# A four-layer graph network on one core: the deviation as exp(-0.5 ln v), two layers normalised on GpSimd, another beginning and another end

## The chip, the core and the metric

The kernel runs on one core of a Trainium2 chip. The core has a matrix engine (TensorE, PE in the profile), a vector engine (VectorE, DVE), an engine for functions of one element (ScalarE, ACT), a general engine (GpSimd, POOL), and a queue (SyncE, SP) that issues most of the transfers between the chip's main memory and the on-chip memories: SBUF, 128 partitions wide, and PSUM, where matrix products arrive. Each engine works through its own list of instructions in order; semaphores make one engine wait for another. The metric is the device time of one execution in microseconds (us), lower is better. Most executions agree within 0.3%.

## The reference, cut to what matters

Thirty-two graphs `x[b]` of 512 nodes with 128 features go through four layers with one shared adjacency matrix. Every layer adds its result to its input and normalises each node's 128 features.

```python
def _layernorm(x, axis=-1, eps=1e-5):
    m = jnp.mean(x, axis=axis, keepdims=True)
    v = jnp.var(x, axis=axis, keepdims=True)
    return (x - m) / jnp.sqrt(v + eps)

# layers 0 and 1: attention over neighbours
h = x @ W
e = leaky_relu((h @ a_src)[i] + (h @ a_dst)[j], 0.2)
out = softmax(where(adj > 0, e, -big)) @ h        # 0: + b, leaky_relu(0.3);  1: elu
# layer 2: own features times W[0], mean over the other neighbours times W[1], + bias
# layer 3: y = (adj @ x + x) @ weight + bias;  y = y / max(norm(y), 1e-12)

x = _layernorm(x + L0(x)); x = _layernorm(x + L1(x))
x = _layernorm(x + L2(x)); x = _layernorm(x + L3(x))
```

## The kernel before, in words

A graph is one tile of 128 partitions by 512 elements: four quarters ("chunks", `NCH` = 4) of 128 nodes, each 128 by 128. The work on a graph is cut into *units*, small functions that issue one or a few instructions on one engine. `@unit("nrm0", ...)` gives a unit's name and its tiles.

The order of everything is written out by hand. `PLAN` gives for each unit and each of the 32 graphs a position (-1: not run), `STARTS` does it for the units that run once. The units are issued in the order of these positions, which interleaves many graphs; an engine's own list is what of it falls to that engine. Tiles come from pools of fixed size (six PSUM banks, thirty SBUF tiles `sq`), in turn.

The steps of a graph, with their lines in the profile:

- `ld` (L150) loads the graph. Its transpose is made on PE with `pt0` (L167) and copied from PSUM with `xt0` (L171), which before does for graph 0 only; for graphs 1 to 31 `lb` (L156) loads it a second time in blocks of 32 by 32, four transfers per graph, and `tr0` (L160) transposes the blocks on DVE.
- Layers 0 and 1: `ph` (L179) multiplies by W and the attention vectors, `ex` (L183) takes exponentials on ACT, `h` (L189) scales. The row of exponentials gets to all partitions either through PE (`pr`, L209, for graphs 0, 1, 2, 30 and 31) or through main memory (`rt`, `rw`, `rb`, L214 to L224). `al` (L236) makes the attention matrix on DVE with four instructions of 128x512, `po` (L196) multiplies on PE, `rs`, `v0`, `v1`, `lr`, `exp`, `elu` finish.
- Layers 2 and 3: `xh`, `xl` (L273 on ACT, L277 on POOL) split the features in two parts, `py` (L284) aggregates, `y` (L288) copies, `po2`, `po3` (L298, L299, L311) multiply by the weights, `v2`, `v3` (L305, L315) add the bias on DVE. In layer 3, `sq` (L321) takes squares and their sums on ACT, `ssp` (L325, L326) takes the maximum with 1e-24 and the power -0.5 on POOL, `rr0` to `rr3` (L333) scale and add the input on DVE.
- Normalising: `add0`, `add1` (L267) and `xb` (L292) are additions on POOL. `bn` takes statistics on DVE (L340, L342): mean and variance plus eps of each node. `ms` (L346) changes the mean's sign on ACT, `pw` (L350, L351) takes the power -0.5 of the variance on POOL and multiplies it by the negative mean, and `nrm` (L356) applies scale and shift on ACT, one instruction for each chunk.
- `st` (L361) stores the graph with one transfer.

Units that run once prepare the masks (`e`, `am`, `m`, `mp`, `cva`, `cvd`, L439 to L473), weights (`awt`, `awc`, `awq`, `aws`, L418 to L433; `wb` loads those of layer 1), biases (`rest`, L412), and warm PE with transposes that nobody reads (`warm`, `warm2`, L401, L406). `de` (L500 to L502) compares the values of the row `eb`, and `out_d` (L507 to L512) collects doubts about the inputs; if there are any, a general path runs at the end, which here does not happen.

Of the kernel before, what the change touches and what calls it, by code (L numbers as in the profile page):

```python
# [14 lines left out]
AF = mybir.ActivationFunctionType  # L15
# [3 lines left out]
P = 128  # L19
# [7 lines left out]
def kernel(  # L27
# [120 lines left out]
    @unit("ld", "x0")  # L148
    def _(b, x0):
        nc.sync.dma_start(chunks(x0), x[b].rearrange("(c p) f -> p c f", p=P))  # L150
# [11 lines left out]
    for k in range(3):  # L162

        @unit(f"pt{k}", f"x{k}", f"pt{k}")
        def _(b, xk, p):
            for c in range(NCH):
                nc.tensor.transpose(p[:, c * P : (c + 1) * P], xk[:, c * P : (c + 1) * P], ident)  # L167

        @unit(f"xt{k}", f"pt{k}", f"xt{k}")
        def _(b, p, xt):  # L170
            nc.scalar.copy(xt, p)  # L171
# [151 lines left out]
    @unit("ssp", "ss")  # L323
    def _(b, ss):
        nc.gpsimd.tensor_scalar(ss, ss, 1e-24, None, op0=ALU.max)  # L325
        nc.gpsimd.tensor_tensor(ss, ss, mhalf, op=ALU.pow)  # L326
# [8 lines left out]
    for k in range(4):  # L335
# [8 lines left out]
        @unit(f"ms{k}", f"mv{k}")  # L344
        def _(b, mv):
            nc.scalar.mul(mv[:, :, 0], mv[:, :, 0], -1.0)  # L346

        @unit(f"pw{k}", f"mv{k}", f"rn{k}")
        def _(b, mv, rn):
            nc.gpsimd.tensor_tensor(rn[:, 0], mv[:, :, 1], mhalf, op=ALU.pow)  # L350
            nc.gpsimd.tensor_mul(rn[:, 1], mv[:, :, 0], rn[:, 0])  # L351
# [6 lines left out]

    @unit("st", "x4")
    def _(b, x4):  # L360
        nc.sync.dma_start(out[b].rearrange("(c p) f -> p c f", p=P), chunks(x4))  # L361

    for n in ("aw0", "aw1", "aq0", "aq1", "pf", "pm0", "pm1", "pm2", "pm3", "pflag"):
        KIND[n] = "ps"
# [10 lines left out]
    def first():  # L375
# [6 lines left out]
        nc.scalar.activation(bad[:, 0:1], minus1, AF.Exp)  # L382
# [15 lines left out]
    @unit("warm", "pf")  # L398
    def _(b, p):
        for i in range(12):  # L400
            nc.tensor.transpose(p[:, :P], ident, ident)  # L401

    @unit("warm2", "pf")
    def _(b, p):
        for i in range(8):
            nc.tensor.transpose(p[:, :P], ident, ident)  # L406
# [112 lines left out]
    def _(b, p):  # L519
# [3 lines left out]
        "ja": 1, "warm": 2, "wb": 3, "awt0": 4, "warm2": 5, "awc0": 6, "e2": 7, "e0": 10, "rest": 11, "am2": 12,  # L523
        "e1": 13, "awq0": 14, "aws0": 16, "am0": 17, "e3": 18, "eh": 20, "am1": 21, "awt1": 22, "am3": 23,
        "awc1": 24, "m2": 26, "m3": 27, "awq1": 29, "m0": 30, "m1": 31, "cva2": 33, "aws1": 34, "mp": 35, "cva1": 38,
        "cvd2": 39, "de": 42, "cva3": 45, "cvd1": 46, "cvd3": 48, "cva0": 51, "cvd0": 54, "dga": 55, "deg": 61,
        "lpp": 239, "lpd": 274, "dv": 420, "out_d": 2455, "out_p": 2530, "out_c": 2533,
    }
    PLAN = {
        "ld": [0, 8, 9, 49, 52, 89, 137, 181, 215, 292, 362, 432, 502, 563, 642, 724, 797, 860, 928, 1006, 1070, 1163,  # L530
            1211, 1280, 1378, 1438, 1526, 1601, 1694, 1944, 1770, 1839],
        "pt0": [15, -1, -1, -1, -1, -1, -1, -1, -1, -1, -1, -1, -1, -1, -1, -1, -1, -1, -1, -1, -1, -1, -1, -1, -1, -1,
            -1, -1, -1, -1, -1, -1],
        "xt0": [19, -1, -1, -1, -1, -1, -1, -1, -1, -1, -1, -1, -1, -1, -1, -1, -1, -1, -1, -1, -1, -1, -1, -1, -1, -1,
            -1, -1, -1, -1, -1, -1],
        "ph0a": [32, 64, 73, 91, 117, 129, 201, 249, 309, 348, 419, 483, 561, 669, 741, 831, 906, 980, 1059, 1143,
            1215, 1298, 1388, 1479, 1568, 1664, 1723, 1797, 1890, 1957, 2059, 2121],
        "ph0b": [25, 60, 67, 94, 116, 125, 175, 218, 263, 345, 415, 486, 562, 670, 713, 775, 864, 929, 1020, 1103,
            1190, 1270, 1351, 1441, 1500, 1569, 1697, 1749, 1830, 1905, 1995, 2086],
        "ex0a": [36, 69, 77, 95, 122, 144, 203, 256, 316, 353, 424, 491, 564, 675, 748, 835, 912, 984, 1064, 1147,  # L540
            1221, 1304, 1397, 1483, 1576, 1671, 1730, 1804, 1894, 1966, 2064, 2130],
        "ex0b": [37, 65, 72, 97, 120, 131, 183, 232, 277, 349, 423, 492, 567, 678, 719, 785, 873, 936, 1025, 1107,
            1195, 1274, 1359, 1451, 1509, 1575, 1700, 1759, 1835, 1913, 1999, 2091],
        "pc0": [43, 75, 80, 101, 123, 148, 204, 264, 322, 356, 427, 497, 570, 683, 751, 837, 915, 992, 1066, 1153,
            1226, 1309, 1401, 1489, 1581, 1673, 1736, 1809, 1899, 1968, 2068, 2133],
        "pr0": [40, 70, 79, -1, -1, -1, -1, -1, -1, -1, -1, -1, -1, -1, -1, -1, -1, -1, -1, -1, -1, -1, -1, -1, -1, -1,
            -1, -1, -1, -1, 2076, 2136],
        "h0a": [47, 76, 81, 102, 124, 153, 206, 265, 328, 357, 429, 499, 572, 684, 752, 843, 916, 1000, 1072, 1157,
            1265, 1339, 1432, 1490, 1584, 1683, 1741, 1822, 1903, 1970, 2069, 2141],
        "h0b": [50, 78, 82, 104, 133, 160, 205, 278, 330, 361, 440, 505, 574, 688, 758, 850, 945, 1005, 1076, 1159,  # L550
            1227, 1310, 1403, 1492, 1587, 1688, 1747, 1829, 1911, 1972, 2081, 2158],
        "al0": [44, 74, 87, -1, -1, -1, -1, -1, -1, -1, -1, -1, -1, -1, -1, -1, -1, -1, -1, -1, -1, -1, -1, -1, -1, -1,
            -1, -1, -1, -1, 2083, 2151],
        "po0a": [58, 85, 96, 178, 197, 240, 301, 358, 405, 534, 575, 617, 698, 800, 872, 952, 1038, 1120, 1206, 1284,
            1368, 1453, 1528, 1607, 1701, 1774, 1846, 1952, 2022, 2096, 2166, 2238],
        "po0b": [53, 90, 109, 185, 189, 234, 312, 363, 396, 545, 585, 639, 734, 807, 878, 983, 1060, 1150, 1224, 1318,
            1394, 1486, 1540, 1650, 1725, 1786, 1871, 1940, 2034, 2111, 2185, 2258],
        "rs0a": [66, 92, 110, 187, 210, 251, 310, 369, 448, 550, 590, 646, 726, 812, 886, 974, 1051, 1136, 1238, 1302,
            1382, 1465, 1550, 1621, 1709, 1777, 1865, 1961, 2030, 2107, 2176, 2247],
        "rs0b": [59, 98, 127, 192, 211, 252, 326, 383, 418, 558, 597, 649, 746, 818, 899, 995, 1077, 1164, 1239, 1334,  # L560
            1409, 1498, 1551, 1662, 1737, 1796, 1882, 1953, 2049, 2126, 2199, 2279],
        "v0a": [68, 99, 114, 190, 214, 259, 311, 374, 455, 554, 592, 666, 731, 819, 901, 979, 1086, 1141, 1243, 1307,
            1387, 1469, 1553, 1623, 1717, 1782, 1870, 1963, 2032, 2108, 2181, 2253],
        "v0b": [71, 103, 130, 198, 216, 262, 327, 394, 458, 573, 609, 668, 753, 827, 904, 997, 1088, 1168, 1245, 1340,
            1413, 1503, 1556, 1669, 1743, 1800, 1887, 1977, 2052, 2128, 2204, 2285],
        "lr": [86, 107, 136, 207, 227, 270, 329, 409, 464, 586, 658, 722, 762, 846, 907, 1018, 1091, 1173, 1248, 1366,
            1416, 1521, 1591, 1674, 1765, 1814, 1934, 1997, 2071, 2139, 2214, 2291],
        "add0": [88, 112, 143, 213, 235, 282, 342, 425, 476, 594, 665, 733, 779, 859, 917, 1021, 1102, 1188, 1275,
            1377, 1433, 1525, 1599, 1686, 1769, 1827, 1943, 2008, 2088, 2143, 2222, 2305],
        "bn0": [93, 118, 156, 222, 245, 300, 379, 430, 490, 612, 687, 739, 815, 887, 954, 1037, 1123, 1203, 1315, 1389,  # L570
            1460, 1538, 1616, 1711, 1778, 1860, 1955, 2020, 2097, 2161, 2237, 2323],
        "ms0": [100, 132, 163, 228, 260, 304, 388, 439, 504, 620, 690, 749, 820, 892, 965, 1045, 1134, 1219, 1342,
            1398, 1467, 1545, 1645, 1718, 1787, 1868, 1960, 2033, 2104, 2167, 2250, 2330],
        "pw0": [105, 135, 166, 229, 266, 307, 390, 445, 509, 623, 691, 754, 822, 896, 970, 1047, 1138, 1222, 1349,
            1402, 1470, 1547, 1654, 1722, 1790, 1883, 1969, 2060, 2112, 2173, 2261, 2333],
        "nrm0": [113, 145, 174, 236, 281, 320, 402, 453, 517, 632, 701, 768, 828, 905, 988, 1057, 1152, 1230, 1353,
            1420, 1476, 1552, 1659, 1733, 1795, 1895, 1978, 2073, 2123, 2180, 2269, 2340],
        "pt1": [121, 151, 194, 247, 296, 331, 411, 471, 544, 645, 711, 778, 869, 962, 1044, 1117, 1200, 1294, 1363,
            1434, 1522, 1811, 1699, 1753, 1852, 1937, 2018, 2122, 2196, 2192, 2293, 2349],
        "xt1": [128, 155, 196, 257, 302, 337, 417, 479, 546, 651, 712, 788, 876, 969, 1052, 1121, 1205, 1299, 1371,  # L580
# [462 lines left out]
```

## Time and profile before

| | |
|---|---|
| time, median of 3 runs | 582.84 us (580.44 to 582.96) |
| the profiled execution | 582.73 us |
| its span, first to last instruction | 581.0 us |
| busy: PE, DVE, ACT, POOL | 547.7, 526.0, 503.6, 427.0 us |
| POOL's powers (L350) | 128 of 1053 ns, 134.7 us |
| ACT's normalisations (L356) | 512, 209.5 us |
| table loads on ACT | 1, 1283 ns |
| PE's last instruction ends | 566.5 us |

A row of the profile names a line of the kernel, its engine and operation, the tiles (`out<-in`) and the shape; "x128" is the number of instructions. Busy time counts overlapping instructions once. "Idle before" is time in which the engine stood still just before such an instruction, and the arrow names what ended it. The profile is of one execution, so sums are made against its span.

### The profile page before, as it was taken

To read this page: it belongs to the slowest core of one execution; us is meant where nothing else is said; L and a number is where in the kernel's file an instruction comes from. 1 tells how busy PE (TensorE), PEld (TensorE's weight loads), DVE (VectorE), ACT (ScalarE), POOL (GpSimd) and SP (SyncE) were. 2 spreads that over 40 slices of the span, in tenths; PEclk is the share of its full clock that TensorE was granted. 3 is DMA by queue.
4 is the path that set the end of the run, shared out by engine and by line. 5 is a ranking of instruction groups with operands and counts; after the bars stand their busy time and mean duration, and the time that the engine had idled before them with its cause. 6 is when DMAs were issued, how large, how long until landed. Compare 5 with 4: busy or idle time off the path is not lost.

```text
span 581.0 us, 13866 instructions
## 1 busy us (share of the span) xinstructions
PE 547.7 (94%) x4200; PEld 516.1 (89%) x4200; DVE 526.0 (91%) x2005; ACT 503.6 (87%) x1653; POOL 427.0 (73%) x578
## 2 busy tenths in 40 slices
PE   7799999899999999999999999999999999999980
PEld 6689999899999999999999989898998999998860
DVE  2688979899999999999998999999999999779674
ACT  4555598798989899999999889899988999998996
POOL 3151685787868787777878579776887779789985
PEclk9788999999999999999999999999999999999995
DMA  6616022323434334352432343332201111000013
GB/s 188 130 38 128 19 60 70 92 65 83 99 77 101 77 70 110 92 117 55 104 78 76 83 97 74 66 101 73 75 20 38 55 38 38 20 2 20 1 37 113
DMA packets 111296, 41.84 MB, mean 72 GB/s; under 512 B 69872, under 2 KB 103792, under 8 KB 111216
## 3 DMA queue, kind: packets, MB, share of 16 engines
q1 hardware_dynamic: 110640, 40.57, 29.2%
q8 instruction: 35, 0.57, 0.4%
q14 instruction: 45, 0.37, 0.2%
q10 hardware_dynamic: 576, 0.33, 0.2%
HBM read 32.38 MB, written 8.50 MB: 70 GB/s over the span
## 4 chain that ended last, share of the span: by engine, by line
DVE 35%; PE 33%; ACT 16%; POOL 5%; SPq 4%; issue 3%; DMA 2%; ACTq 0%; DVEq 0%; POOLq 0%
PE ps L196 16%; DVE al L236 12%; ACT sq L356 8%; PE ps L284 7%; DVE st L340 6%; PE ps L179 4%; DVE sq L333 3%; DVE sq L305 2%; SPq L156 2%; DVE mv L342 2%; DVE sq L243 2%; ACT hp L189 2%; PE ps L167 2%; PE ps L311 2%; DVE sq L253 2%
## 5 line engine op out<-in xcount | busy, mean ns | idle before, releaser
L196 PE MATMUL ps<-hp,al 128*128 128x129 f32 x2048 | 251.2, 279 | 6.4 <-DVE al L236 4.4
L196 PEld LDWEIGHTS ps<-hp,al 128*128 128x128 f32 x2048 | 243.1, 195 | 10.0 <-issue 3.1
L356 ACT ACTIVATE sq<-sq,rn 128x128 f32<-128x128 f32 x512 | 209.5, 492 | 12.8 <-POOL rn L351 12.6
L350 POOL TENSOR_TENSOR rn<-mv,mhalf 128x4 f32<-128x4 f32 x128 | 134.7, 1053 | 22.1 <-DVE mv L342 15.4
L236 DVE SCALAR_TENSOR_TENSOR al<-rb,exps,mp 128x512 f32<-128x512 f32 x216 | 145.5, 734 | 1.6 <-DMA rb<-rd 1.5
L340 DVE BATCH_NORM_STATS2 st<-sq 128x6 f32<-128x128 f32 x512 | 109.0, 273 | 4.2 <-POOL sq L267 4.1
L277 POOL TENSOR_TENSOR xr<-sq,xr 128x512 fp32r<-128x512 f32 x64 | 83.1, 1302 | 15.1 <-ACT xr L273 13.5
L189 ACT ACTIVATE hp<-ps,exps 128x128 f32<-128x128 f32 x256 | 87.8, 421 | 0.2
L179 PE MATMUL ps<-we,sq 128*128 128x131 f32 x512 | 73.5, 277 | 3.1 <-ACT sq L171 2.0
L179 PEld LDWEIGHTS ps<-we,sq 128*128 128x128 f32 x512 | 66.0, 190 | 5.9 <-ACT sq L171 2.6
L284 PE MATMUL ps<-off,xr 128*128 128x512 f32 x256 | 67.3, 405 | 1.8 <-ACT hp L189 1.5
L284 PE MATMUL ps<-a3t,xr 128*128 128x512 f32 x256 | 67.2, 405 | 0.7 <-ACT sq L249 0.7
L284 PEld LDWEIGHTS ps<-off,xr 128*128 128x128 f32 x256 | 45.7, 188 | 11.4 <-ACT hp L189 1.9
L284 PEld LDWEIGHTS ps<-a3t,xr 128*128 128x128 f32 x256 | 45.9, 188 | 10.2 <-ACT sq L249 1.0
L267 POOL TENSOR_TENSOR sq<-sq,x 128x512 f32<-128x512 f32 x32 | 42.3, 1323 | 15.6 <-DVE sq L253 10.4
L292 POOL TENSOR_TENSOR sq<-sq,bias_b 128x512 f32<-128x512 f32 x32 | 41.6, 1300 | 14.3 <-ACT sq L356 11.6
L333 DVE SCALAR_TENSOR_TENSOR sq<-sq,ss,sq 128x128 f32<-128x128 f32 x128 | 47.6, 413 | 3.7 <-POOL ss L326 3.6
L267 POOL TENSOR_TENSOR sq<-sq,sq 128x512 f32<-128x512 f32 x32 | 41.7, 1306 | 11.3 <-DVE sq L261 10.6
L298 PE MATMUL ps<-w,sq 128*128 128x128 f32 x256 | 49.5, 275 | 0.0
L299 PE MATMUL ps<-w,sq 128*128 128x128 f32 x256 | 49.5, 275 | 0.0
L342 DVE BATCH_NORM_AGGREGATE mv<-st 128x2 f32<-128x9 f32 x512 | 48.9, 155 | 0.0
L171 ACT COPY sq<-ps 128x512 f32<-128x512 f32 x65 | 37.8, 584 | 11.2 <-PE ps L167 10.9
(91 smaller groups left out, 832.9 us busy)
## 6 DMA issues: line engine op xcount, KB each, us to landing
rb<-rd SPq DMA_DIRECT2D x54, 256.0 KB
x<-in_x_dram SPq DMA_DIRECT2D x32, 256.0 KB
out_dram<-sq SPq DMA_DIRECT2D x32, 256.0 KB
sw<-in_x_dram SPq DMA_DIRECT2D x124, 64.0 KB
rd<-rt SPq DMA_DIRECT2D x216, 0.5 KB
an<-in_adj_dram SPq DMA_DIRECT2D x3, 256.0 KB
an<-in_adj_dram ACTq DMA_DIRECT2D x1, 256.0 KB
w<-in_L_gnn_W_dram SPq DMA_DIRECT2D x2, 64.0 KB
```

What stands on the lines that cost most here:

```text
L179: nc.tensor.matmul(twos(p)[:, c, :FE], xt[:, (2 * half + c) * P : (2 * half + c + 1) * P], ATT[k], start=True, stop=True)
L189: nc.scalar.activation(h[:, 2 * half + c, :F], twos(p)[:, c, :F], AF.Identity, bias=pc if k else 0.0, scale=pc)
L196: nc.tensor.matmul(twos(p)[:, c, : F + 1], al[:, j, rows], h[:, j, :], start=(j == 0), stop=(j == NCH - 1))
L236: nc.vector.scalar_tensor_tensor(al[:, j, :], r, exps[:, 2 * b + k, 2, j : j + 1], mask[:, j, :], op0=ALU.max, op1=ALU.mult)
L267: nc.gpsimd.tensor_add(o, o, xk)
L277: nc.gpsimd.tensor_sub(xl, xk, xh.bitcast(F32))
L284: nc.tensor.matmul(p, part[:, j * P : (j + 1) * P], mat[:, j, :], start=(i + j == 0), stop=(i + j == NCH))
L333: nc.vector.scalar_tensor_tensor(o[:, cols], o[:, cols], ss[:, c : c + 1], x3[:, cols], op0=ALU.mult, op1=ALU.add)
L340: nc.vector.bn_stats(st[:, c, :6], o[:, c * P : (c + 1) * P])
L342: nc.vector.bn_aggr(mv[:, c, :], st[:, c, :])
L350: nc.gpsimd.tensor_tensor(rn[:, 0], mv[:, :, 1], mhalf, op=ALU.pow)
L356: nc.scalar.activation(xo[:, c * P : (c + 1) * P], o[:, c * P : (c + 1) * P], AF.Identity, bias=rn[:, 1, c : c + 1], scale=rn[:, 0, c : c ...
```

## The change

1. *The deviation.* `ms`, `pw` and `ssp` go. `le` and `lx` take exp(-0.5 ln v) with two small ACT instructions, `nm` multiplies by the negative mean on DVE. For layer 3's norm, `sm` takes the maximum on DVE, `sle` and `slx` do the rest on ACT. At the start, one table of ACT that has both functions is loaded by name.
2. *Layers 0 and 2* are normalised with `nrm0p`, `nrm2p`: per chunk one GpSimd instruction, times scale plus shift. Layers 1 and 3 stay on ACT.
3. *The beginning.* Graphs 0 to 3 are loaded one after the other and transposed on PE (`pt0`, `xt0`); the second load and DVE's transpose are for graphs 4 to 31 only. `warm2` goes; `de` moves from position 42 to 431; `wb` and `rest` come after the loads of graphs 1 to 3.
4. *The end.* Layer 3 of graphs 30 and 31 runs by chunks from `po3` to the store: `po3c`, `v3c`, `sqc`, `smc`, `slc`, `sxc`, `rrc`, `bnc`, `lec`, `lxc`, `nmc`, then `nrc` on ACT for chunks 0 and 2, `nvc` on DVE for 1 and 3, and `stc`. The copy from PSUM is shared by ACT and DVE (`y3x`, `y3y`).
5. The positions of all units are new; 2,913 units are issued instead of 2,648.

```diff
-    @unit("ssp", "ss")
+    @unit("sm", "ss")
     def _(b, ss):
-        nc.gpsimd.tensor_scalar(ss, ss, 1e-24, None, op0=ALU.max)
-        nc.gpsimd.tensor_tensor(ss, ss, mhalf, op=ALU.pow)
+        nc.vector.tensor_single_scalar(ss, ss, 1e-24, op=ALU.max)
+
+    @unit("sle", "ss")
+    def _(b, ss):
+        nc.scalar.activation(ss, ss, AF.Ln)
+
+    @unit("slx", "ss")
+    def _(b, ss):
+        nc.scalar.activation(ss, ss, AF.Exp, scale=-0.5)
...
-        @unit(f"ms{k}", f"mv{k}")
-        def _(b, mv):
-            nc.scalar.mul(mv[:, :, 0], mv[:, :, 0], -1.0)
-
-        @unit(f"pw{k}", f"mv{k}", f"rn{k}")
+        @unit(f"le{k}", f"mv{k}", f"rn{k}")
         def _(b, mv, rn):
-            nc.gpsimd.tensor_tensor(rn[:, 0], mv[:, :, 1], mhalf, op=ALU.pow)
-            nc.gpsimd.tensor_mul(rn[:, 1], mv[:, :, 0], rn[:, 0])
+            nc.scalar.activation(rn[:, 1], mv[:, :, 1], AF.Ln)
+
+        @unit(f"lx{k}", f"rn{k}")
+        def _(b, rn):
+            nc.scalar.activation(rn[:, 0], rn[:, 1], AF.Exp, scale=-0.5)
+
+        @unit(f"nm{k}", f"mv{k}", f"rn{k}")
+        def _(b, mv, rn):
+            nc.vector.scalar_tensor_tensor(rn[:, 1], mv[:, :, 0], -1.0, rn[:, 0], op0=ALU.mult, op1=ALU.mult)
...
+        @unit(f"nrm{k}p", f"o{k}", f"rn{k}", f"x{k + 1}")
+        def _(b, o, rn, xo):
+            for c in range(NCH):
+                nc.gpsimd.tensor_scalar(xo[:, c * P : (c + 1) * P], o[:, c * P : (c + 1) * P], rn[:, 0, c : c + 1],
+                                        rn[:, 1, c : c + 1], op0=ALU.mult, op1=ALU.add)
+
+    @unit("y3x", "py3", "y3")
+    def _(b, p, y):
+        nc.scalar.copy(y[:, : 2 * P], p[:, : 2 * P])
+
+    @unit("y3y", "py3", "y3")
+    def _(b, p, y):
+        nc.vector.tensor_copy(y[:, 2 * P :], p[:, 2 * P :])
+
+    for c in range(NCH):
+        cols = slice(c * P, (c + 1) * P)
+
+        @unit(f"po3c{c}", "y3", "po3")
+        def _(b, y, p, cols=cols):
+            nc.tensor.matmul(p[:, cols], y[:, cols], w3_s, start=True, stop=True)
+
+        @unit(f"v3c{c}", "po3", "o3")
+        def _(b, p, o, cols=cols):
+            nc.vector.tensor_tensor(o[:, cols], p[:, cols], bias3_b, op=ALU.add)
...
+        @unit(f"nrc{c}", "o3", "rn3", "x4")
+        def _(b, o, rn, xo, c=c, cols=cols):
+            nc.scalar.activation(xo[:, cols], o[:, cols], AF.Identity, bias=rn[:, 1, c : c + 1], scale=rn[:, 0, c : c + 1])
+
+        @unit(f"nvc{c}", "o3", "rn3", "x4")
+        def _(b, o, rn, xo, c=c, cols=cols):
+            nc.vector.tensor_scalar(xo[:, cols], o[:, cols], rn[:, 0, c : c + 1], rn[:, 1, c : c + 1], op0=ALU.mult, op1=ALU.add)
+
+        @unit(f"stc{c}", "x4")
+        def _(b, x4, c=c, cols=cols):
+            nc.sync.dma_start(out[b, c * P : (c + 1) * P, :], x4[:, cols])
...
-        nc.scalar.activation(bad[:, 0:1], minus1, AF.Exp)
+        nc.scalar.add_instruction(mybir.InstLoadActFuncSet(name=nc.get_next_instruction_name(), act_func_set_id=6))
...
     STARTS = {
-        "ja": 1, "warm": 2, "wb": 3, "awt0": 4, "warm2": 5, "awc0": 6, "e2": 7, "e0": 10, "rest": 11, "am2": 12,
+        "ja": 1, "warm": 2, "wb": 6, "awt0": 7, "awc0": 8, "e2": 10, "awq0": 11, "e0": 13, "am2": 15, "aws0": 16,
...
     PLAN = {
-        "ld": [0, 8, 9, 49, 52, 89, 137, 181, 215, 292, 362, 432, 502, 563, 642, 724, 797, 860, 928, 1006, 1070, 1163,
+        "ld": [0, 3, 4, 5, 12, 108, 127, 178, 246, 319, 398, 463, 535, 625, 682, 774, 834, 936, 990, 1055, 1139, 1212,
...
```

The units left out, `sqc` to `nmc`, are those of `sq` to `nm` with one chunk's columns. In the list of PE after the change stand, in this order: `warm`, `awt0`, `pt0.0`, `awq0`, `am2`, `am0`, `ph0b.0`, `am1`, `ph0a.0`, `am3`, `awt1`, `pt0.1`, `pt0.2`, `awq1`, `pr0.0`.

## The prediction

> **What bounds the kernel now.** I read the page first (busy shares, then the span in slices).
>
> ```profile
> PE 547.7 (94%) x4200; PEld 516.1 (89%) x4200; DVE 526.0 (91%) x2005; ACT 503.6 (87%) x1653; POOL 427.0 (73%) x578
> ...
> PE   7799999899999999999999999999999999999980
> ...
> DVE  2688979899999999999998999999999999779674
> ACT  4555598798989899999999889899988999998996
> ```
>
> TensorE (PE) and VectorE (DVE) are full through the middle, ScalarE (ACT) nearly. An average hides where each has room, so I cut the span into beginning, middle and end; after the length of a stretch stand the busy us of PE, weight load, DVE, ACT, POOL (GpSimd):
>
> ```profile
> 0.00:60.00 60.00, 51.06 (x358) 47.86 (x359) 40.50 (x115) 29.95 (x93) 17.88 (x48) 0.89 0.52 117
> 60.00:500.00 440.00, 433.14 (x3416) 411.31 (x3415) 426.83 (x1625) 399.94 (x1319) 343.12 (x446) 1.00 0.31 73
> 500.00:581.00 81.00, 63.46 (x432) 56.93 (x430) 58.69 (x268) 73.69 (x242) 65.99 (x84) 0.92 0.11 31
> ```
>
> PE idles 8.9, 6.9 and 17.5 us; DVE 19.5, 13.2 and 22.3 (together 55.0, and 526.0 + 55.0 = 581.0). So the middle can't become shorter unless PE and DVE get less work, which neither does here. What can be won is idle time at the ends. The timeline shows the first:
>
> ```profile
> 14.24 0.42 DVE L500 TENSOR_REDUCE ends<-eb 128x1 f32<-128x256 f32 x1 [2.15 <-DMA eb<-in_L_gnn_e_dram]
> ...
> 15.28 2.72 DVE L236 SCALAR_TENSOR_TENSOR al<-ps,exps,mt 128x512 f32<-128x512 f32 x4
> ...
> 25.13 2.73 DVE L236 SCALAR_TENSOR_TENSOR al<-ps,exps,mt 128x512 f32<-128x512 f32 x4 [0.55 <-PE ps L209]
> ```
>
> DVE waits for the row `eb`, which nothing urgent needs, before the first attention matrix; graph 1's follows 10 us later. At the end PE is done at 566.5, DVE at 573.6, the last normalisation at 577.3, and the last store has landed by 581.0.
>
> The groups that the change touches (busy us, mean ns of one | idle before):
>
> ```profile
> L356 ACT ACTIVATE sq<-sq,rn 128x128 f32<-128x128 f32 x512 | 209.5, 492 | 12.8 <-POOL rn L351 12.6
> L350 POOL TENSOR_TENSOR rn<-mv,mhalf 128x4 f32<-128x4 f32 x128 | 134.7, 1053 | 22.1 <-DVE mv L342 15.4
> L342 DVE BATCH_NORM_AGGREGATE mv<-st 128x2 f32<-128x9 f32 x512 | 48.9, 155 | 0.0
> ```
>
> L342's mean is 155 ns, but 48.9/512 is 96 ns: neighbours on DVE overlap by some 60 ns. A resource that matters below shows in the source view of L333 (min/median/max ns) and in two pieces of the timeline:
>
> ```profile
> L333 DVE SCALAR_TENSOR_TENSOR sq<-sq,ss,sq x128: 302/343/1446, 121.9 to 572.0; 128x128 f32<-128x128 f32 x128
> ```
>
> ```profile
> 526.86 1.29 POOL L292 TENSOR_TENSOR sq<-sq,bias_b 128x512 f32<-128x512 f32 x1
> ...
> 527.77 0.40 DVE L511 SCALAR_TENSOR_TENSOR bad<-bad 128x1 f32<-128x1 f32 x1
> ```
>
> L511 has one element per partition, yet it ends (528.17) only when POOL's add does (528.15).
>
> **What the Trainium skill says.** (1) SBUF — State Buffer, Who interferes with whom: a DVE instruction with two SBUF inputs contends with a GpSimd instruction that reads SBUF, and the later one blocks. L511 and L333's 1446 ns agree. (2) ScalarE: Activation LUTs, Table sets: one set holds exp and ln, so they can alternate without a reload (1283 ns for the one load of before); no run shows ln yet. (3) GPSIMD Engine Reference, Performance versus the Vector engine: two tensor inputs cost some 2.5 cycles per element, a short one-input body 1.03. The trace agrees: 128x128 with two inputs took 452 ns (L462), with one 301 (L383).
>
> **The change, part by part.** The sum is made against the profiled execution: span 581.0, and 1.73 outside, make its 582.73 us, 0.11 below the median of the runs, 582.84.
>
> *GpSimd.* Out: 128 powers (134.7), their products (L351, 31.2), the norm's maximum and power (8.1 + 33.8). In: 256 scale-and-shifts of 128x128, a form with two per-partition scalars that nothing here shows: between L383's 301 and L462's 452 ns. I take 310, since one tensor is streamed: 79. POOL falls to 298 (335 at the upper price). Four take 1.24 us (1.81), against 209.5/512 x 4 = 1.64 on ACT, so no chain grows. Behind them in POOL's queue stand the `xl` subtractions that PE's aggregation waits for; POOL, half idle, covers that.
>
> *ScalarE.* Out: 256 normalisations, 104.7, and 128 sign changes, 26.7. In: 344 small ln and exp at 0.2 (L346, 128x4, took 212 ns), 69; three copies, 1.7. ACT falls to about 442. That shortens its queue: ACT is busy 73.7 of the last 81 us, where PE and DVE stand idle.
>
> *DVE, the account that decides.* In: 134 products `nm`. A tensor_tensor of one element took 158 ns (L512); less the overlap, 95: 12.7 (21 if nothing overlaps). 38 maxima at 95: 3.6. Two graphs by quarters: eight bias additions of 278 (L315's 678 less 384 elements at 0.96 per ns) for two of 678, +0.9; two half copies +0.8; four normalisations +1.1. Out: three 32x32 transposes, 2.1. `nm` has two SBUF inputs, so it meets the lock; L333 (mean 413, median 343) loses 70 ns each to it. From below 0, from above 9.4; I take 7, because POOL's adds remain. Sum: 526.0 + 12.7 + 3.6 + 2.8 - 2.1 + 7 = 550.0. DVE now carries more than PE.
>
> *PE.* Twelve transposes of 152 ns more (1.8), eight warm-up ones less (1.9, in idle time): unchanged, 547.6.
>
> *Beginning.* `de` leaves, graphs 0 to 3 are loaded straight and transposed on PE, twelve `lb` issues leave SP's queue (5.50 us for 8). But graphs 1 to 3 are loaded ahead of layer 1's weights, and PE's queue has W1's transpose (`awt1`) in front of `pr0.0`, DVE's has `awc1` and `aws1` in front of the first attention matrix. The bytes ahead of W1 come to 2.1 MB; at the 188 GB/s of the first slice it lands near 12 us, or 13.5. So that cover is gone: I put the first attention matrix at 14.5 instead of 15.28, with graphs 1 and 2 right behind. DVE idle in the first 60 us: 10.9 (3.6 busy before) + 3.3 = 14.2, against 19.5. Without `warm2`, if PE kept the clock of 0.74 for 5 us longer, 1.3 more; I take 0, since PE gets dense work sooner.
>
> *End.* The last two graphs run by quarters, each stored when ready. Six more store issues at 0.44 stand on SP, with only stores behind. After DVE's last instruction a store alone is left (577.3 to 581.0, some 4), and I give 4.5 to hops between ACT and DVE: idle 8.5, against 22.3.
>
> *New waits.* `nm` waits for ACT's exp, `sm` for ACT's square (POOL did before). DVE is in order: attention matrices, bias additions and statistics stand behind them, and PE behind those. DVE's waits on ACT today (L214, 54 instructions, 2.7 us; L261, 32, 0.5) come to 37 ns each; 172 new ones at that price are 6.4. Against that its waits on PE (11.7 at L200, 4.6 at L305, 3.3 at L315) go as DVE becomes the later one. From 150 to 300 us, where DVE was the fuller, it idled 1.8 of 150; 1.2% of 440 is 5, which I take for the middle, against 13.2.
>
> Span: 550.0 + 14.2 + 5 + 8.5 = 577.7; time 579.4, say 579.
>
> **Rivals.** *Slower by round trips and the lock.* Statistics, ln, exp, product: DVE, ACT, DVE, 126 times, in DVE's queue from 60 to 500 us. The forecast gains 3.8; it is used up when each of the 172 waits costs 22 ns more than allowed, or when the lock takes 0.08 us per product instead of 0.05. At 70 ns more it ends at 591. For: DVE had 3% of slack there. Against: ACT goes from 91% busy in the middle to about 80% and answers sooner.
>
> *Cancelled.* `nm` without overlap (+8), or the middle as idle as before (+8), with half of one: 583.
>
> *PE stays the bound.* DVE's extra work falls into its idle time; PE idles 5, 7 and 10: 547.6 + 22 + 1.7 = 571. For: PE is 98.4% busy in the middle, DVE 97.0. Against: 550 us on DVE leave it hardly less to do than that.
>
> *Not what it says.* ln and exp reload tables each time: 344 x 1.28, +440, some 1020. Against: one explicit load of one set.
>
> **Numbers.** Forecast (574 to 580): 0.36; PE-bound (567 to 574): 0.09; cancelled (580 to 586): 0.22; slower (586 to 600): 0.32; reloads: 0.01. A measurement of this kernel tells 0.5%, 2.9 us, from no change. Faster 0.45, same 0.22, slower 0.33. The range 569 to 594 leaves out a third of the PE-bound case, about 0.1 of the slow one and the reloads.
>
> **What would show it.** ACT near 440 and POOL near 300 us busy; DVE near 550 and over 98% in the middle; the first L236-like row near 14.5 us; DVE idle under 10 us after 500; one table load. It is wrong if the `nm` rows have a mean well over 200 ns or more than 10 us of idle before them, if the scale-and-shift takes over 452 ns, or if PE starts before 12 us.

## The result and the profile after

The changed kernel takes 603.33 us (median of four, 599.03 to 605.48) against 581.98 for the kernel before beside it (580.44 to 582.96): ratio 1.036, 95% interval 1.030 to 1.042. The forecast was 579, its range 569 to 594. The profiled execution is the lowest of the four: 599.03 us, span 597.3.

The page's busy times of the changed kernel:

```profile
PE 553.2 (93%) x4204; PEld 515.6 (86%) x4204; DVE 563.6 (94%) x2186; ACT 443.5 (74%) x1611; POOL 342.4 (57%) x514
```

ACT came out as forecast (442 said, 443.5 found) and PE nearly so (547.6, 553.2). DVE has 13.6 us more than the 550.0 of the account, POOL 44 more than the 298. The same cut into beginning, middle and end as before; after the length of a stretch stand the busy us of PE, weight load, DVE, ACT and POOL:

```profile
0.00:60.00 60.00, 54.60 (x436) 52.01 (x437) 44.65 (x147) 33.83 (x110) 22.70 (x62) 1.00 0.44 108
60.00:500.00 440.00, 419.45 (x3241) 393.07 (x3241) 436.98 (x1665) 329.52 (x1189) 269.65 (x389) 1.00 0.29 70
500.00:597.30 97.30, 79.19 (x530) 70.48 (x528) 82.01 (x377) 80.16 (x314) 50.02 (x65) 0.91 0.14 40
```

DVE is busy 436.98 of 440 us in the middle: it alone sets the pace there, and PE, which idled 6.9 us in this stretch before, now idles 20.5. DVE's idle time is 15.35 + 3.0 + 15.3 us (forecast 14.2, 5 and 8.5). Against the forecast span of 577.7 that makes +13.6 of work, +1.1 at the beginning, -2.0 in the middle and +6.8 at the end, together the 19.6 us that the profiled span is longer. The median lies another 4.3 above the profiled execution.

The groups of the changed kernel that answer to those shown of before (busy us, mean ns of one | idle before):

```profile
L372 POOL TENSOR_SCALAR sq<-sq,rn 128x128 f32<-128x128 f32 x256 | 117.6, 476 | 65.2 <-DVE rn L361 42.4
L366 ACT ACTIVATE sq<-sq,rn 128x128 f32<-128x128 f32 x248 | 102.1, 485 | 26.3 <-DVE rn L361 25.9
L340 DVE SCALAR_TENSOR_TENSOR sq<-sq,ss,sq 128x128 f32<-128x128 f32 x120 | 53.1, 474 | 0.4 <-ACT ss L333 0.4
L353 ACT ACTIVATE rn<-mv 128x4 f32<-128x4 f32 x126 | 25.4, 205 | 35.9 <-DVE mv L349 18.3
```

L340 is the scaled addition `rr`, L333 in the kernel before; its mean went from 413 to 474 ns. The scale-and-shift L372 has a mean of 476 ns, above the bracket of 301 to 452. The new product `nm` is L361:

```profile
L361 DVE SCALAR_TENSOR_TENSOR rn<-mv,rn x126: 111/150/2350, 30.8 to 584.9; 128x4 f32<-128x4 f32 x126
```

The median of these products over four numbers per partition is 150 ns, the longest 2350. I call a stall what an instruction takes above the median of its group, if that is over 60 ns. Summed over DVE, stalls are 14.2 us in the kernel before (9.7 in `rr`, 11 of 128 instructions) and 38.3 in the changed one: 16.1 in `nm` (29 of 126), 16.4 in `rr` (17 of 120), 2.3 in the maximum `sm` (L325, 7 of 30), the rest in L253 and L261. The timeline around the longest:

```profile
196.91 2.54 POOL L277 TENSOR_TENSOR xr<-sq,xr 128x512 fp32r<-128x512 f32 x2
...
197.11 2.35 DVE L361 SCALAR_TENSOR_TENSOR rn<-mv,rn 128x4 f32<-128x4 f32 x1
...
199.50 0.49 ACT L366 ACTIVATE sq<-sq,rn 128x128 f32<-128x128 f32 x1 [2.72 <-DVE rn L361]
```

The product starts inside one of GpSimd's subtractions, ends at 199.46 with the next one (199.45), and ACT's normalisation has waited 2.72 us for it. Of the 29 stalled products 20 end within 0.12 us of an addition or subtraction of 1.2 us or more (15.1 of the 16.1 us); eight overlap a scale-and-shift alone (0.8 us), one meets both. The loss is uneven: told apart by their positions in `PLAN`, the 64 products of layers 0 and 2 lost 4.4 us, the 62 of layers 1 and 3 lost 11.6.

### The profile page after: what moved, and what is told of

It is laid out like the page before. It is cut to its first block, busy times and chain, and to the rows that moved or that the text cites. A ratio compares the mean times of both kernels' runs of the same rounds, so it can differ in the third digit from the quotient of the medians.

```text
span 597.3 us, 13877 instructions
## 1 busy us (share of the span) xinstructions
PE 553.2 (93%) x4204; PEld 515.6 (86%) x4204; DVE 563.6 (94%) x2186; ACT 443.5 (74%) x1611; POOL 342.4 (57%) x514
## 5 line engine op out<-in xcount | busy, mean ns | idle before, releaser
L196 PE MATMUL ps<-hp,al 128*128 128x129 f32 x2048 | 246.6, 275 | 2.7 <-ACT hp L189 0.9
L196 PEld LDWEIGHTS ps<-hp,al 128*128 128x128 f32 x2048 | 237.9, 191 | 7.6 <-DVE al L236 2.0
L372 POOL TENSOR_SCALAR sq<-sq,rn 128x128 f32<-128x128 f32 x256 | 117.6, 476 | 65.2 <-DVE rn L361 42.4
L366 ACT ACTIVATE sq<-sq,rn 128x128 f32<-128x128 f32 x248 | 102.1, 485 | 26.3 <-DVE rn L361 25.9
L347 DVE BATCH_NORM_STATS2 st<-sq 128x6 f32<-128x128 f32 x504 | 107.5, 272 | 4.5 <-POOL sq L267 4.5
L277 POOL TENSOR_TENSOR xr<-sq,xr 128x512 fp32r<-128x512 f32 x64 | 82.5, 1294 | 8.0 <-ACT xr L273 8.0
L267 POOL TENSOR_TENSOR sq<-sq,sq 128x512 f32<-128x512 f32 x32 | 41.8, 1306 | 68.8 <-DVE sq L261 40.9
L284 PE MATMUL ps<-a3t,xr 128*128 128x512 f32 x256 | 68.4, 411 | 0.5 <-DVE sq L243 0.5
L249 ACT ACTIVATE sq<-ps,rs 128x128 f32<-128x128 f32 x128 | 39.6, 366 | 31.1 <-DVE rs L200 31.0
L267 POOL TENSOR_TENSOR sq<-sq,x 128x512 f32<-128x512 f32 x32 | 42.0, 1314 | 26.3 <-DVE sq L253 18.0
L284 PEld LDWEIGHTS ps<-a3t,xr 128*128 128x128 f32 x256 | 47.3, 193 | 10.6 <-DVE sq L243 0.7
L292 POOL TENSOR_TENSOR sq<-sq,bias_b 128x512 f32<-128x512 f32 x32 | 41.3, 1290 | 23.6 <-ACT sq L366 17.7
L340 DVE SCALAR_TENSOR_TENSOR sq<-sq,ss,sq 128x128 f32<-128x128 f32 x120 | 53.1, 474 | 0.4 <-ACT ss L333 0.4
L353 ACT ACTIVATE rn<-mv 128x4 f32<-128x4 f32 x126 | 25.4, 205 | 35.9 <-DVE mv L349 18.3
```

The lines of the kernel that those rows point to most:

```text
L196: nc.tensor.matmul(twos(p)[:, c, : F + 1], al[:, j, rows], h[:, j, :], start=(j == 0), stop=(j == NCH - 1))
L267: nc.gpsimd.tensor_add(o, o, xk)
L277: nc.gpsimd.tensor_sub(xl, xk, xh.bitcast(F32))
L284: nc.tensor.matmul(p, part[:, j * P : (j + 1) * P], mat[:, j, :], start=(i + j == 0), stop=(i + j == NCH))
L340: nc.vector.scalar_tensor_tensor(o[:, cols], o[:, cols], ss[:, c : c + 1], x3[:, cols], op0=ALU.mult, op1=ALU.add)
L347: nc.vector.bn_stats(st[:, c, :6], o[:, c * P : (c + 1) * P])
```

## The experiments

Theory A: what was mis-priced is the lock between GpSimd and a DVE instruction with two SBUF inputs, at `nm` above all. Rival B: the chain DVE, ACT, DVE costs the time by waits. Rival C: GpSimd's new scale-and-shift is what locks, and the old place of layers 0 and 2 was better. Rival D: the new order, its beginning or its end cost the time. Each group of runs has the kernel before beside it; its medians are 581.7 to 582.1.

**The product with one input.** The instruction stays, but writes only the negative mean; the multiplication by the scale is left out.

```diff
-            nc.vector.scalar_tensor_tensor(rn[:, 1], mv[:, :, 0], -1.0, rn[:, 0], op0=ALU.mult, op1=ALU.mult)
+            nc.vector.tensor_reduce(rn[:, 1], mv[:, :, 0:1], axis=AX.X, op=ALU.add, negate=True)
```

> The changed kernel, with nm reading one tensor instead of two: it writes the negative mean and leaves out the product by the deviation, so the numbers that come out are not those of the reference; waits, place and length of the instruction stay. If the lock that DVE shares with GpSimd is what nm costs, the 16 us by which nm instructions exceed their median of 150 ns go: DVE busy falls from 563.6 to about 548 and the time from 603 to 587-591. If it is the number of nm instructions and their waits on ACT, DVE stays at 560 or more and the time at 600-605; the same if the new order of the units is the cause.

585.85 us (583.70 to 587.11), ratio to before 1.006 (1.004 to 1.008): 17.5 us less than the changed kernel. DVE is busy 549.8 instead of 563.6, its stalls are 25.9 us instead of 38.3, none of them at the product (104 to 158 ns). This speaks for A, with a gap: this product does not read the exponential, so it need not wait for it. The reduction over a pair, below, closes it.

**No product in layers 0 and 2.** GpSimd subtracts the mean and multiplies by the scale, `nm` stays in layers 1 and 3.

```diff
-                nc.gpsimd.tensor_scalar(xo[:, c * P : (c + 1) * P], o[:, c * P : (c + 1) * P], rn[:, 0, c : c + 1],
-                                        rn[:, 1, c : c + 1], op0=ALU.mult, op1=ALU.add)
+                nc.gpsimd.tensor_scalar(xo[:, c * P : (c + 1) * P], o[:, c * P : (c + 1) * P], mv[:, c, 0:1],
+                                        rn[:, 0, c : c + 1], op0=ALU.subtract, op1=ALU.mult)
```

> The changed kernel, with layers 0 and 2 normalised on GpSimd as (x - mean) times scale, so that nm is needed for layers 1 and 3 only: 64 of 126 whole nm instructions go. DVE account: 64/126 of nm's 33.2 us busy, so DVE falls to about 547 and the time to 586-590. If the order of the units is the cause: 600 or more. GpSimd's own busy time should stay at 342.

609.88 us (609.26 to 613.60), ratio 1.050 (1.046 to 1.054). Half of the products are gone and the time rose; the other form of the same instruction turned out much dearer on GpSimd:

```profile
L373 POOL TENSOR_SCALAR sq<-sq,mv,rn x256: 782/792/2783, 30.8 to 586.4; 128x128 f32<-128x128 f32 x128
```

792 ns against 454, GpSimd busy 436.9 instead of 342.4; the 62 remaining products lost 11.7 us in 17 stalls and `rr` 19.1. So the run tells nothing of the product alone: 600 or more was to be the sign of the order, but the dearer instruction is a cause as well. Nor did a busier GpSimd stall the products more: the same 62 products, those of layers 1 and 3, lost 11.6 us in the changed kernel. The half that is gone had only 4.4 us of stalls, so the expectation counted too much gain for it.

**Layers 0 and 2 on ACT again.**

```diff
-                nc.gpsimd.tensor_scalar(xo[:, c * P : (c + 1) * P], o[:, c * P : (c + 1) * P], rn[:, 0, c : c + 1],
-                                        rn[:, 1, c : c + 1], op0=ALU.mult, op1=ALU.add)
+                nc.scalar.activation(xo[:, c * P : (c + 1) * P], o[:, c * P : (c + 1) * P], AF.Identity, bias=rn[:, 1, c : c + 1],
+                                     scale=rn[:, 0, c : c + 1])
```

> The changed kernel, with layers 0 and 2 normalised on ACT again, in the same order of units. ACT goes to about 548 us busy, GpSimd to 225. If the scale-and-shift instructions are what locks DVE out, DVE loses some 20 us of stalls and the time falls to 585. If the long two-input additions are, as the stalls that met only a scale-and-shift (13 of 56) say, DVE falls by 5-10 and the time is 593-600, or stays because ACT is full again.

640.35 us (638.87 to 642.00), ratio 1.099 (1.097 to 1.101). With no scale-and-shift on GpSimd at all, the stalls are still 33.7 us, 15.2 of them at `nm` (26 of 126) and 14.8 at `rr`. So C falls as to the lock: the additions and subtractions of 1.3 us, which the kernel before has too, hold it. In the changed kernel the 13 stalls that met a scale-and-shift and no addition or subtraction are 1.6 us of the 38.3. The time went up by something else. What PE waited for in this run (us in total, times, longest):

```profile
PE ps L311 <- ACT sq L288: 18.3, 15, 3.3
PE ps L179 <- ACT sq L171: 16.0, 11, 3.2
```

ACT, with 534.4 us of work in an order made for 443, brings its copies late, and DVE falls to 403.9 of 440 us in the middle. DVE's own largest wait in this run is the product's for the exponential, 18.1 us in 19 waits: B does cost time where ACT is late. Whether layers 0 and 2 would be better on ACT in an order made for that is left open.

**The old deviation in the new order.** As the run before, and the powers back on GpSimd, `ms` on ACT, no `nm`, `sm`, logarithm or exponential but for the quarters of graphs 30 and 31: about the engine loads of the kernel before with the new order, beginning and end.

```diff
-            nc.scalar.activation(rn[:, 1], mv[:, :, 1], AF.Ln)
+            nc.scalar.mul(mv[:, :, 0], mv[:, :, 0], -1.0)
+            nc.gpsimd.tensor_tensor(rn[:, 0], mv[:, :, 1], mhalf, op=ALU.pow)
+            nc.gpsimd.tensor_mul(rn[:, 1], mv[:, :, 0], rn[:, 0])
...
-            nc.scalar.activation(rn[:, 0], rn[:, 1], AF.Exp, scale=-0.5)
-            nc.vector.scalar_tensor_tensor(rn[:, 1], mv[:, :, 0], -1.0, rn[:, 0], op0=ALU.mult, op1=ALU.mult)
```

> The changed kernel, with the deviation by GpSimd's power again (sign on ACT, maximum and power of the norm on GpSimd) and layers 0 and 2 on ACT, for all but the four chunks of graphs 30 and 31; new order, beginning and end stay. DVE account: nm and sm leave DVE, 563.6 - 33 - 7 = 524, time 575-583. If the order, the beginning or the end is the cause: 595 or more.

631.97 us (629.59 to 632.15), ratio 1.084 (1.082 to 1.087), although DVE has only 533.6 us and stalls of 16.6. A time of 595 or more was to be the sign of D, and it came. But the run can't tell a bad order from one used with loads that it was not written for, so it neither shows D nor rules it out; I take it for such a misfit, as in the run before. The later runs therefore change as little of the loads as they can.

**The product on GpSimd.**

```diff
             nc.scalar.activation(rn[:, 1], mv[:, :, 1], AF.Ln)
+            nc.gpsimd.tensor_scalar(mv[:, :, 0], mv[:, :, 0], -1.0, None, op0=ALU.mult)
...
-            nc.vector.scalar_tensor_tensor(rn[:, 1], mv[:, :, 0], -1.0, rn[:, 0], op0=ALU.mult, op1=ALU.mult)
+            nc.gpsimd.tensor_mul(rn[:, 1], mv[:, :, 0], rn[:, 0])
```

> The product of mean and deviation leaves VectorE: GpSimd turns the mean's sign beside ScalarE's logarithm and multiplies after the exponential. Lock theory: with it go its 33.2 us of busy time (own work and stalls), so VectorE falls from 563.6 to about 532; with the 33.7 us of idle time of the changed kernel that is 566 and TensorE with its 20 us of idle is 570; time 565 to 575. Rival (the price is the chain through three engines, not the lock): the product stands behind 1.3 us additions in GpSimd's queue, every normalisation is later, VectorE and TensorE wait for it, time 585 or more, though VectorE is less busy.

591.00 us (589.59 to 593.10), ratio 1.017 (1.012 to 1.021). It is 12.3 us quicker than the changed kernel, but misses the 565 to 575 of A by far: by its number the rival of this run, the chain through three engines, holds. ACT waits 32.2 us (29 times) for the product here, and 15.0 (27 times) in the run below that keeps it on DVE as a reduction. The middle of it:

```profile
60.00:500.00 440.00, 425.27 (x3304) 401.59 (x3303) 427.46 (x1608) 336.90 (x1223) 322.67 (x600) 1.00 0.29 72
```

DVE, without the products, idles 12.5 us here instead of 3.0, and PE 14.7: neither is full, both wait for data. And a part of the stalls only moved; the maximum `sm`, which lost 2.3 us in the changed kernel, lost 8.0 (11 of 30):

```profile
L325 DVE TENSOR_SCALAR ss<-ss x30: 122/161/2128, 115.6 to 572.5; 128x4 f32<-128x4 f32 x30
```

**The maximum on GpSimd too.**

```diff
-        nc.vector.tensor_single_scalar(ss, ss, 1e-24, op=ALU.max)
+        nc.gpsimd.tensor_scalar(ss, ss, 1e-24, None, op0=ALU.max)
```

> As the run with the product on GpSimd, and the norm's maximum on GpSimd too (30 of 128x4). Lock theory: the 30 rows of the maximum (7.0 us busy with 2.3 to 5.0 of stalls) leave VectorE, 3 to 6 us less than that run. Rival: the maximum's stalls only go to the next instruction (the sums of the last layer), less than 1 us.

590.44 us (589.52 to 590.99), ratio 1.015 (1.012 to 1.019): DVE went from 544.1 to 533.1 us busy and the time by 0.6, which these intervals do not tell from nothing. The stalls did not go to `rr`, where the rival of this run sent them (14.2 us in the run before, 13.2 here). Instead DVE idles 9.8 us more, 5.7 of them before `rr`, which waits for the norm: its maximum now stands in GpSimd's queue, and ACT waits 7.3 us for it. So the run is no pure test of less work on DVE; it shows work moved off DVE that came back as waiting.

**The end of the last two graphs whole.**

```diff
+    for g in (30, 31):
+        for whole, parts in (("y3", ("y3y",)), ("po3", ("po3c0", "po3c1", "po3c2", "po3c3")),
...
+                             ("st", ("stc0", "stc1", "stc2", "stc3"))):
+            PLAN[whole][g] = max(PLAN[n][g] for n in parts)
...
+                PLAN[n][g] = -1
```

> The changed kernel with graphs 30 and 31 ended whole, each stage where its last quarter stood. Theory (quarters bring what the end won): idle of VectorE after 500 us goes from 15.3 back towards 22, less 2.8 us of extra work: 606 to 610. Rival (quarters cost as much in small instructions and hops as they save): 600 to 604.

598.42 us (596.29 to 602.26), ratio 1.029 (1.022 to 1.036): not longer, as the quarters were supposed to save, but 4.9 us shorter than with quarters. The two intervals overlap, so this pair only says that the quarters do not save several us; the pair without the maximum, below, is sharper.

**The kernel before with the row `eb` read later.**

```diff
-        "cvd2": 39, "de": 42, "cva3": 45,
+        "cvd2": 39, "de": 415, "cva3": 45,
```

> The kernel before with the reductions of the edge row moved from place 42 to 415, nothing else. Theory (the wait for that row holds the first attention matrix): its first attention row starts 0.5 to 1 us sooner and the time falls by 0 to 1 us. Rival (matrix and weights come no sooner, or the ends of the span set the time): no change, within 0.3 us.

580.91 us (577.21 to 582.48, 20 runs), ratio 0.9981 (0.9968 to 0.9995). The mask copies and the first attention matrix in this run, which stood at 10.61 and 15.28 us:

```profile
9.23 1.29 DVE L449 COPY mt<-ps 128x512 f32<-128x512 f32 x2
...
12.14 2.73 DVE L236 SCALAR_TENSOR_TENSOR al<-ps,exps,mt 128x512 f32<-128x512 f32 x4 [1.43 <-PE ps L209]
```

The matrix starts 3.1 us sooner, more than I thought. But 1.4 of that was there at the mask copies already, which stand ahead of `de` in both kernels: PE's mask transposes took 276 ns in this execution, 310 in the one before. So `de` accounts for some 1.8 us, and 1.1 us reach the end. This is the only version here below the kernel before, by 0.2%, with an interval that just leaves out 1.

**The product as a reduction over a pair.** The exponential is written where the variance stood, beside the mean; the shift is minus the product over that pair, read as one input.

```diff
-            nc.scalar.activation(rn[:, 0], rn[:, 1], AF.Exp, scale=-0.5)
+            nc.scalar.activation(mv[:, :, 1], rn[:, 1], AF.Exp, scale=-0.5)
...
-            nc.vector.scalar_tensor_tensor(rn[:, 1], mv[:, :, 0], -1.0, rn[:, 0], op0=ALU.mult, op1=ALU.mult)
+            nc.vector.tensor_reduce(rn[:, 1], mv, axis=AX.X, op=ALU.mult, negate=True)
```

> The whole computation, with the product as a reduction over the pair (mean, scale): one SBUF input, and it waits for the exponential as the changed kernel's product does. Lock theory (two SBUF inputs are what it costs): as the run with the product by one input, 584 to 588, VectorE busy near 550. Rival (that run was quick because its product, without the deviation, waited for no exponential): 594 or more, with the time in idle before the product.

587.18 us (586.19 to 587.95), ratio 1.0095 (1.006 to 1.013): 16.1 us less than the changed kernel, as A said, with the same work on the same engine in the same place behind the same exponential. The source view of the product:

```profile
L361 DVE TENSOR_REDUCE rn<-mv x126: 108/146/164, 29.7 to 572.2; 128x4 f32<-128x8 f32 x126
```

The median stays (150, now 146), the longest falls from 2350 to 164 ns. This agrees with the Trainium skill, SBUF — State Buffer, section Who interferes with whom, which says that `tensor_reduce` never contends on trn2. The idle time before the products is 1.7 us in 4 waits here and 2.0 in 5 in the changed kernel, so B is worth at most 2 us at the product itself; what the longer chain costs further on, this pair does not tell.

**The norm's floor in the logarithm.** As that run, `sm` and its quarters gone; the logarithm adds 1e-24.

```diff
-        nc.vector.tensor_single_scalar(ss, ss, 1e-24, op=ALU.max)
...
-        nc.scalar.activation(ss, ss, AF.Ln)
+        nc.scalar.activation(ss, ss, AF.Ln, bias=tiny)
```

> As the run with the reduction over the pair, and the norm's maximum gone from VectorE: the floor of 1e-24 is added in the logarithm. VectorE is the bound: its 38 maxima (7 to 10 us busy with stalls) go and a hop with them, 577 to 581. Rival (TensorE or the hops bound it by now): less than 2 us below that run.

583.21 us (580.24 to 585.32, 20 runs), ratio 1.0026 (1.0011 to 1.0041). 4.0 less, between the 6 to 10 that I expected and the less than 2 of the rival. DVE is busy 544.0 instead of 550.1, and its stalls, 26.0 us with the reduction, are 21.5: the 5.0 of the maximum left, of which 0.5 went to `rr` (18.0).

**The same with whole ends.** The edit of the whole end, on top of this.

> As the run without the maximum, graphs 30 and 31 ended whole. Theory from the whole-end run of the changed kernel (598.4 against 603.3: quarters cost): 2 to 5 us less than with quarters. Rival (that difference was scatter of the stalls; the quarters save 2 to 4 us): 2 to 4 us more.

583.11 us (580.33 to 585.85, 20 runs), ratio 1.0028 (1.0012 to 1.0044): no difference that these intervals show, against both sides of the expectation. The ends of the two, quarters first (the stretch is cut past the end of both spans):

```profile
500.00:640.00 140.00, 62.36 (x404) 55.15 (x402) 62.76 (x290) 65.16 (x260) 38.27 (x49) 0.93 0.07 20
```

```profile
500.00:640.00 140.00, 61.91 (x402) 54.69 (x400) 59.12 (x270) 63.86 (x240) 38.48 (x48) 0.94 0.07 20
```

The spans end at 580.4 and 579.1, so DVE has 62.76 us of work and 17.6 of idle with quarters, 59.12 and 20.0 whole: the quarters win 2.4 us of waiting and cost about as much in small instructions (3.6 in this stretch, 3.1 over the span).

**The last layer's sum left in PSUM.** On top of that, in 23 of 32 graphs, `v3` writes its sum back into the bank and `rr` reads it there.

```diff
-            nc.vector.scalar_tensor_tensor(o[:, cols], o[:, cols], ss[:, c : c + 1], x3[:, cols], op0=ALU.mult, op1=ALU.add)
+            nc.vector.scalar_tensor_tensor(o[:, cols], p[:, cols], ss[:, c : c + 1], x3[:, cols], op0=ALU.mult, op1=ALU.add)
```

> As the run without the maximum and with whole ends; in 23 of 32 graphs (all whose banks allow it) the last layer's sum stays in PSUM, so that the scaled addition L340 reads one operand from PSUM and one from SBUF. Lock theory: 92 of its 128 instructions lose their stalls, some 13 of 18 us; VectorE 540.9 to about 528, TensorE's 547 with its idle bounds it: 570 to 576. Rival (the PSUM banks are held longer, TensorE waits for a free one): 583 or more with TensorE's idle up, though VectorE has 528.

588.87 us (584.17 to 589.53), ratio to the 581.68 beside it 1.010 (1.008 to 1.013). The lock half of the expectation came true in kind (all stalls together fell from 21.7 to 12.2 us, by 9.5 where some 13 were expected), the time did not. The two forms of `rr` in this run, from PSUM and from SBUF:

```profile
L358 DVE SCALAR_TENSOR_TENSOR sq<-ps,ss,sq x92: 303/340/352, 121.4 to 580.5; 128x128 f32<-128x128 f32 x92
L341 DVE SCALAR_TENSOR_TENSOR sq<-sq,ss,sq x36: 305/343/1369, 154.2 to 481.0; 128x128 f32<-128x128 f32 x36
```

The same operation and shape: 92 with one operand from PSUM, none over 352 ns; 36 with both from SBUF, nine of them stalled, up to 1369. The two forms differ in the place of one input alone, so it is the second SBUF input that the stalls of `rr` hang on. DVE fell to 532.8 us. But what it waited for most now reads:

```profile
DVE rs L201 <- PE ps L197: 11.6, 13, 4.0
```

That row stood at 2.1 us in 3 waits in the run that this one is built on. PE idles 14.2 us in the middle instead of 9.4. The six banks are held longer, which is the rival that I wrote down; that PE waits for a bank is inferred from this, the waits name only the producers of its data.

## Why the prediction was wrong

**The lock term failed.** The account of DVE took 7 us for the lock at the products, with 9.4 as the upper end. Stalls rose by 24.1 (14.2 to 38.3): 16.1 at `nm`, 6.7 at `rr`, 2.3 at `sm`, and 1.0 less at L253. The other terms of the account came out 3.5 us lower than I had them together (563.6 less 24.1 is 539.5, the account without its lock term 543.0), so DVE has 13.6 more. With the lock taken from `nm` alone, the time falls by 16.1 of the 24.3 us by which the forecast missed. That DVE is then busy 550.1 us, the forecast's number, is luck: it still holds 11.8 us of stalls more than the kernel before where 7 were taken, and the other terms were too high.

How the bound was made is the mistake. I took the average loss of `rr`, 70 ns, for the most that `nm` could lose. But that average held 11 stalls in 128, from an instruction that in the kernel before can start only when GpSimd has finished a power for it. A fairer price of a small instruction is the share of the span in which the other engine holds the port, times what is left of it, half its instruction on average: GpSimd's additions and subtractions in the kernel before (L277 83.1, L267 42.3 and 41.7, L292 41.6 us) are 36% of 581, and half of 1.3 us is 0.65. 126 products would lose 29 us if they fell at random; they lost 16.1, 0.127 each. The same estimate gives `rr` in the kernel before 30 us, and it lost 9.7. So it is a price from above, too high by a factor of two to three here, but with 16.1 inside it, and it could be made from the page of the kernel before.

**The stalls of `rr` and `sm`** were not in the lock term at all. That `rr` lost more because it no longer follows GpSimd's power directly is argued, not shown: in the new order with the power on GpSimd it lost 12.9 us, between the two. For `sm` the same section of the skill would have warned: it counts `tensor_scalar` among the forms that can take both ports where their operands allow it. Whether `sm` did is not shown, but its 30 instructions, one input each, took up to 1219 ns, and up to 2128 with the products on GpSimd.

**The end** was given 8.5 us of idle time and has 15.3. After DVE's last instruction 4.3 us remain (4 said); the hops took 11.0 instead of 4.5, of them 2.6 on PE, 2.1 on GpSimd and 2.0 on ACT's exponential. The quarters themselves save 2.4 us of idle time (20.0 whole, 17.6 in quarters, in the pair without the maximum), where the forecast went from 22.3 to 8.5, and their small instructions cost as much.

**The scale-and-shift** took 454 ns at the median (310 taken, 452 the upper end). That is the time of L462 with two tensors (452), though only one tensor is streamed here; the prediction's reason for 310 failed, and why is not known. (The page that it names there, GPSIMD Engine Reference, gives about 2.6 cycles for two inputs in the section Performance versus the Vector engine, not 2.5; the bracket came from the trace and does not rest on it.) GpSimd, at 57%, bears it; what it adds to the lock is the 1.6 us of stalls that met it alone.

**The beginning** was nearly right: 15.35 us of DVE's idle time for 14.2, the first attention matrix at 15.59 us instead of 14.5, with seven more of its rows right behind. What was late is in the timeline:

```profile
12.76 1.29 DVE L528 COPY mt<-ps 128x512 f32<-128x512 f32 x2 [3.88 <-PE ps L523]
...
15.59 2.07 DVE L236 SCALAR_TENSOR_TENSOR al<-ps,exps,mt 128x512 f32<-128x512 f32 x3 [0.29 <-ACT sq L171]
```

DVE waits 3.88 us for PE's mask transposes, 16 of 423 ns (310 before), and W1's small instructions follow ahead of the matrix. The prediction had a term for a slower PE without `warm2`, 1.3 us, and put it at nothing. The profiles speak for the term: in all twelve without `warm2` these transposes took 348 to 423 ns on average, in the two with it 276 and 310. Where they took 348 or 349, the first matrix stood at 14.2 and 14.5 us; at 420 or more, at 15.1 to 15.7. The granted clock reads 1.00 in the first 15 us of both kernels, so that column does not tell the two apart. That `warm2` is the reason is not shown: no run puts it back into the new beginning.

**What held.** ACT at 443.5 us with one table load; DVE the bound, at 99.3% in the middle; the waits of `nm` on ACT, 2.0 us in all, less than the 37 ns apiece that were allowed. Of the rival "slower by round trips and the lock" the second half came and the first did not: it was to decide at 0.08 us per product, and 0.127 was measured. Its own 591 was too low, since `rr`, `sm` and the end came on top, and 603.33 lies above the 600 at which that case ended. Of the signs of being wrong that the prediction named, these came: a mean of the `nm` rows well over 200 ns (273), and a scale-and-shift over 452.

**What stays open.** Why `rr` stalls more in the new order, and the products of layers 1 and 3 more than the others; what that order is worth with the engine loads kept equal, since no run here keeps them equal, and with it the 1.2 us that the best version of the change still lies above the kernel before; why the changed kernel scatters by 6 us in four executions where the kernel before scatters by 2.5 in four (5.3 in 38); and whether an order made anew for the one-input product and the late `de` would beat the kernel before.

## What to carry to other kernels

When work is moved onto VectorE while GpSimd runs long two-input instructions, count the moved instructions' SBUF inputs: price two inputs by GpSimd's share of the span times half its instruction, as an estimate from above, however small the moved one is. Then look for a reduction over a pair, or put an operand in PSUM; one input alone is no safeguard, as the maximum shows. Look at what the remedy makes the engine wait for: 11 us less on VectorE moved the time by 0.6 when its work went into GpSimd's queue, and 8 us less on it went with 5.8 us more time when the operand in PSUM was tried. A hand-written order may fit only the engine loads that it was made for: undoing one part of a change inside it can measure the misfit as well.

## What the hardware showed that was not expected

- An instruction of 128x4 took 2350 ns, through one GpSimd subtraction of 1.3 us and the whole next one: VectorE was not let in between the two. In the run without products in layers 0 and 2 one `rr` took 4576 ns and ended 0.15 us after the last of three additions and subtractions in a row.
- GpSimd took 792 ns (782 the least) for subtract-then-multiply with two per-partition scalars on 128x128, and 454 (446 the least) for multiply-then-add on the same shape.
- `tensor_reduce` with one SBUF input was never stalled (164 ns at most in 126), the maximum with an immediate, also with one input, in up to 12 of 30.
- PE's 128x128 transposes in the first 15 us took 421 or 273 ns each at the same granted clock of 1.00, and how long the slow stretch lasted differed between the profiles (the last slow one starts at 3.8 us in the kernel before with a late `de`, at 8.0 in the kernel before, at 13.5 in the changed one).
- Small logarithms and exponentials of 128x4 took 205 to 209 ns each on ACT, and 344 of them (some of 128x1) in turn needed no second table load.
